# A Mamba block in chunks of 2 and 4 tiles, with its projections, gate inputs, norms and table loads moved

## The chip, the cores and the metric

The kernel runs on one core of one Trainium2 chip, in one launch. The metric is the device time in microseconds (us). The time before is 3584.68 us, the median of three runs (3582.42 to 3585.52). A profile of one execution accompanies it. Engines are named as in the profile: PE is TensorE (PEld its weight loads), DVE is VectorE, ACT is ScalarE, POOL is GpSimd and SP is the queue that issues the DMAs.

## The reference

Four graph layers follow each other on 3327 nodes with 256 features; each is `x = layernorm(x + layer(x, adj))`. The first is a mean aggregation, the third graph attention, the fourth two steps of attention that keeps the largest probabilities. The change lies in the second layer, a graph convolution with a Mamba block behind it:

```
h = layernorm(relu(adj @ x @ gcn_w + gcn_b)) * ln_g + ln_b
xz = h @ w_in                             # 512 channels of xc, 512 of z
xc, z = xz[:, :512], xz[:, 512:]
u = silu(causal 4-tap convolution of xc along the nodes + conv_b)
dbc = u @ w_xp                            # 16 columns for dt, 16 for B, 16 for C
dt = softplus(dbc[:, :16] @ w_dt + b_dt)
for t in nodes:                           # state: 512 channels x 16
    state = exp(dt[t] * A) * state + dt[t] * B[t] * u[t]
    y[t] = state @ C[t]
out = (y + u * D_skip) * silu(z) @ w_out
```

The nodes are the steps of the scan, so that the layer is sequential along them. The convolution of the graph, `adj @ x`, is needed for a node before its step.

## The kernel before

Nodes are padded to 26 tiles of 128. In the second layer channels lie on the partitions, in four groups g of 128, and nodes along the free axis. The nodes are taken in chunks c; `ends` (L261) gives chunks of 1, 2 and 3 tiles and then five of 4 tiles (WC = 512 nodes), eight in all. In each chunk there are 16 slots s, one for each of the state's 16 columns. Slot k = 16c + s does, in the loop at L660:

- `decay` (L571): four ACT exponentials dA = exp(dt * A), one per group, into PSUM. There are two buffers, so that a dA waits until the scan two before it has read its own. `in_turn` (L282) keeps these and a number of other ACT operations in the order of the program.
- `scan` (L585): four DVE scans h = dA * h + (dt u B).
- `feed` (L579): one POOL product of dt u and the row of B, made two slots ahead. `row` (L563) loads the rows of B and C from DRAM by SP, three buffers deep.
- `product` (L592): one DVE product hc of h and the row of C, with two buffers.
- `add_up` (L600): PE transposes that add hc into the sums y of each tile in PSUM. They are issued in the next slot.

Beside this a chunk's slots carry the work for its neighbours, at the slots that `plan(c)` (L246) gives. For chunk c+1 the class `Head` has `project(g)` (two matmuls, an ACT copy and the first tap u on ACT), `taps` (three DVE operations for each group, which read what `project` wrote), `silu`, `mixed` (the product with w_xp), `step_size(g)` (a matmul and two ACT operations), `exponentials` and `logarithms` (softplus), `rounding` and `finish` on DVE, and `skip` (u * D_skip on ACT). For the chunk itself, `gate_input` makes z for one tile; SiLU of the gates follows at slot `gsilu`. For chunk c-1, slot 0 gates the sums (DVE), slots 1 to 4 transpose them and add the residual (`gated`, `residual`), slot 6 makes the factors of the layer norm, and slot 13 applies them to the tiles of X in a loop on ACT (L711). With that `ready` allows `value` (L432), which prepares the third layer for a tile of X, to be used as filling work.

SiLU, exponential and logarithm need different tables on ACT. A table load stands in the program before the first operation that needs another table than the one loaded.

The graph's convolution itself is a generator, `convolve` (L308): for each tile 26 matmuls with the adjacency (loaded by SP in pieces, two buffers), then a chain over ACT and PE for weights, relu and norm, whose last steps (`measure`, `norm`, `turn`) are strewn between the matmuls of the following tile. `turn` writes the transposed tile for `project`. `quota` (L408) spreads this stream over the slots: from `duty`, an estimate of PE's work in each slot in units of about a quarter of a 256-column matmul, it fills the slots evenly, so that the tiles of a chunk are through at the slot of its first projection (`due`, L403); `pump` makes up what is missing. When the stream has ended, `value` takes its place.

Before the first slot, tiles for chunk 0 are convolved, `Head(0)` runs at high priority, and the stream goes on to the end of chunk 1. In the slots (`pinned`) DVE and POOL keep the order of the program; PE and the ACT operations outside `in_turn` are ordered by the scheduler by priority when the program is built, and each engine then takes its own operations strictly in that order. PSUM has one buffer each for projections, gates and residuals together (`ps`) and for convolution and values (`cb`).

After the last slot, the last chunk's four tiles are gated, added and normed one after another, with the values between them (L747 to L766).

Of the kernel before, what the change touches and what calls it, by code (L numbers as in the profile page):

```python
# [9 lines left out]
F32 = mybir.dt.float32  # L10
# [37 lines left out]
def gnn_kernel(ctx: ExitStack, tc: tile.TileContext, n: int, a: dict, out: bass.AP):  # L48
# [109 lines left out]
    with tc.tile_pool(name="l1b", bufs=1) as wpool, tc.tile_pool(name="l1at", bufs=2) as l1at:  # L158
# [33 lines left out]
        with tc.tile_pool(name="l1aw", bufs=1) as cwork, tc.tile_pool(name="l1c", bufs=2) as ch, \  # L192
# [53 lines left out]
            def plan(c):  # L246


                if c == 0:
                    return dict(project={0: (0, 1), 1: (2, 3)}, taps={2: (0, 1), 3: (2, 3)}, gates={2: (0,)}, silu=3, gsilu=3,  # L250
                                mixed=5, sizes={6: (0, 1), 7: (2, 3)}, exps=(8, 9), log=11)
                if c == 1:
                    return dict(project={3: (0, 1), 4: (2, 3)}, taps={5: (0, 1), 6: (2, 3)}, gates={5: (0, 1)}, silu=6, gsilu=6,
                                mixed=8, sizes={8: (0,), 9: (1, 2), 10: (3,)}, exps=(10, 11), log=12)
                return dict(project={6: (0, 1), 7: (2, 3)}, taps={7: (0, 1), 8: (2, 3)}, gates={5: (0, 1), 8: (2,), 12: (3,)},
                            silu=8, gsilu=14, mixed=9, sizes={9: (0,), 10: (1, 2), 11: (3,)}, exps=(11, 12), log=13)

            ends = []
            while not ends or ends[-1] < npad:
                prev = ends[-1] if ends else 0  # L260
                ends.append(min(npad, prev + min(WC, (1 + len(ends)) * P)))  # L261
            nch = len(ends)
            starts = [0] + ends[:-1]
            hTs, us, szs, rows_of = {}, {}, {}, {}
# [17 lines left out]
            def in_turn(op, *x, **k):  # L282
                with tc.issue_after(decays[-1].ins) if decays else nullcontext():
                    decays.append(op(*x, **k))  # L284
# [6 lines left out]
            def power(rs, var):  # L291

                gps.tensor_scalar(rs, var, EPS, None, op0=ALU.add)
                gps.tensor_tensor(rs, rs, mhalf[:, :var.shape[1]], op=ALU.pow)

            def spread(y, sm, nm, sq):

# [10 lines left out]
            def convolve():  # L308
# [3 lines left out]
                for it in range(nt):  # L312
                    cb = cpsum.tile([P, 2, D], F32, name="cb")
                    acc, tp = cb[:, 0, :], cb[:, 1, :]
                    for j in range(nt):
                        if j % JC == 0:
                            m = min(JC, nt - j)
                            at = l1at.tile([P, JC, P], F32, name="at")
                            nc.sync.dma_start(at[:, :m, :], a["adjT"][it][:, j:j + m, :])
                        ten.matmul(acc, at[:, j % JC, :], X0[:, j, :], start=(j == 0), stop=(j == nt - 1))  # L320
                        if j % JM == JM - 1 and j < nt - 1:
                            if rest:
                                step = rest.pop(0)
                                step()
                                full += step is turn
                            yield full, 4 * JM
                    m = cwork.tile([P, D], F32, name="m")
                    act.copy(m, acc)
                    yield full, 8
                    for k in range(2):  # L330
                        ten.transpose(tp[:, k * P:(k + 1) * P], m[:, k * P:(k + 1) * P], ident)
                    mt = cwork.tile([P, D], F32, name="m")
                    act.copy(mt, tp)
                    yield full, 4
                    for k in range(2):
                        ten.matmul(acc, mt[:, k * P:(k + 1) * P], gw[:, k, :], start=(k == 0), stop=False)
                    ten.matmul(acc, one, gb, start=False, stop=True)
                    h = cwork.tile([P, D], F32, name="hn")
                    rs, nb, nm, sm, sq = (small.tile([P, 1], F32, name=x) for x in ("rs", "nb", "nm", "sm", "sq"))
                    act.activation(h, acc, AF.Relu, accum_out=sm)  # L340
                    spread(h, sm, nm, sq)

                    def measure(rs=rs, nb=nb, nm=nm, sq=sq):
                        scales(rs, nb, nm, sq)

                    def norm(h=h, rs=rs, nb=nb):
                        in_turn(act.activation, h, h, AF.Identity, scale=rs, bias=nb)

                    def turn(it=it, h=h):
                        c = next(x for x in range(nch) if it * P < ends[x])  # L350
                        i = it * P - starts[c]
                        if i == 0:
                            hTs[c] = ch.tile([P, D // P, WC], F32, name="hT", bufs=3)
                        pt = psum.tile([P, WC], F32, name="ps")
                        for k in range(2):
                            ten.transpose(pt[:, k * P:(k + 1) * P], h[:, k * P:(k + 1) * P], ident)
                        for k in range(2):
                            act.activation(hTs[c][:, k, i:i + P], pt[:, k * P:(k + 1) * P], AF.Identity,
                                                 scale=g1[:, k:k + 1], bias=b1[:, k:k + 1])
                    rest = [*2 * [lambda: None], measure, *2 * [lambda: None], norm, lambda: None, turn]  # L360
                    if not pinned:
                        for step in (measure, norm, turn):
                            step()
                        rest = []
                        full += 1
                    yield full, 14
# [30 lines left out]
            def tiles_of(c):  # L397
                return (ends[c] - starts[c]) // P if 0 <= c < nch else 0
# [261 lines left out]
            for k, (c, s) in enumerate(states):  # L660
# [6 lines left out]
                if s == 0 and c:  # L667
                    plus = [small.tile([P, WC // P], F32, name=f"{x}c")[:, :tiles_of(c - 1)] for x in ("rs", "nb", "nm", "sm", "sq")]
                if added:
                    add_up(*added)  # L670
                for g in range(NG):
                    scan(k, g, dAs.pop(0))
                    if g < 2:
# [23 lines left out]
                    feed(k + 2)  # L697
                if s == 6 and c:
                    scales(plus[0], plus[1], plus[2], plus[4])
                if s == p["gsilu"]:  # L700
                    in_turn(act.activation, szs[c], szs[c], AF.Silu)
                if after:
                    if s == p["silu"]:
                        ahead.silu()
                    elif s == p["log"]:
                        ahead.logarithms()
                    elif s == 15:
                        ahead.skip()
                    if s in p["exps"]:
                        ahead.exponentials(2 * p["exps"].index(s))  # L710
                if c and s == 13:  # L711
                    rs, nb = plus[:2]
                    for i in range(tiles_of(c - 1)):
                        x = X[:, starts[c - 1] // P + i, :]
                        in_turn(act.activation, x, x, AF.Identity, scale=rs[:, i:i + 1], bias=nb[:, i:i + 1])
                    ready = ends[c - 1] // P

                uses = []
                if c and 1 <= s <= tiles_of(c - 1):
# [854 lines left out]
```

## Time and profile before

| what | value |
|---|---|
| time, median of three runs | 3584.68 us |
| profiled execution | 3579.2 us, span 3577.4 us, granted clock 0.96 |
| busy share of the span: PE, DVE, ACT, POOL | 91%, 67%, 49%, 26% |
| second layer, first convolution to last value | 354.6 to 1451.4 us |
| before the first scan | 354.6 to 416.9 us |
| chunks of 1, 2, 3 tiles (16 slots each) | 68.2, 98.1, 123.3 us |
| chunks of 4 tiles | 152.3, 147.2, 146.9, 146.6, 118.2 us |
| after the last product | 34.2 us |

A chunk is taken here from the end of the last product hc before it to the end of its own last product. Matmuls in fp32 stand as two records each, transposes as one; a busy PE is not at its peak, since the ends of matmuls are modelled and overlap. Starts of consecutive operations are closer than their durations on ACT and DVE, by about 0.1 us. In the timeline, the bracket behind a line gives the idle time of the engine before it and what ended it. Many operations of the slots stand under L277 or L284, the lines of the helpers that record them; they are told apart by their tiles: h is a scan or feed, hc a product, dA a decay, u a tap, X a norm.

### The profile page before, as it was taken

Reading aid. Unit: us, or ns where it says so; the run is one execution under the profiler, and the core shown is the slowest. Engines: PE = TensorE matmul, PEld = TensorE weight load, DVE = VectorE, ACT = ScalarE, POOL = GpSimd, SP = SyncE. Lnnn points to the kernel's source line nnn. Section 1 sums busy time; section 2 is a strip of 40 time slices with the busy share of each in tenths; the row PEclk is TensorE's granted clock in tenths of the full one; section 3 lists DMA queues with packets and bytes.
Section 4 is the critical chain, followed back from the end, with each engine's and each line's share of the span. In section 5 each row is a group of like instructions: output and inputs, shape, how many; then the busy total and the mean of one; then the engine's idle time right before and its main releaser. Section 6 shows DMA issues by size and latency. Waiting matters only on the chain. (4 is left out here: it accounts for less than half of the span.)

```text
span 3577.4 us, 43633 instructions
## 1 busy us (share of the span) xinstructions
PE 3268.2 (91%) x15627; PEld 2564.5 (72%) x15627; DVE 2390.6 (67%) x5342; ACT 1758.9 (49%) x2834; POOL 918.2 (26%) x963
## 2 busy tenths in 40 slices
PE   9999888888888765899989999999998899999996
PEld 7888666666666554688867777878776677777775
DVE  1111378799889898677645454444532999999996
ACT  1000576656667674111133333333335888888883
POOL 0000145455655555111100000000001243333332
PEclk9999999998999987899999999999999999999998
DMA  7443344333333222344321211212122122222220
GB/s 246 141 135 103 95 108 116 105 98 106 102 105 98 60 65 47 123 142 148 110 84 49 63 56 56 64 48 66 53 59 75 44 59 69 65 63 69 69 63 17
DMA packets 151996, 308.01 MB, mean 86 GB/s; under 512 B 19858, under 2 KB 73266, under 8 KB 151634
## 3 DMA queue, kind: packets, MB, share of 16 engines
q1 hardware_dynamic: 151762, 305.06, 29.0%
q8 instruction: 126, 2.06, 0.2%
q14 instruction: 108, 0.88, 0.1%
HBM read 294.36 MB, written 10.65 MB: 85 GB/s over the span
## 5 line engine op out<-in xcount | busy, mean ns | idle before, releaser
L277 POOL TENSOR_TENSOR h<-du,row 128x2048 f32<-128x2048 f32 (+3 forms) x126 | 473.6, 3759 | 447.1 <-DVE hc L277 283.5
L277 DVE TENSOR_TENSOR_SCAN h<-dA,carry,h 128x512 f32<-128x512 f32 (+2 forms) x448 | 492.2, 1151 | 51.7 <-ACT dA L284 51.4
L284 ACT ACTIVATE dA<-t,A_log 128x512 f32<-128x512 f32 (+3 forms) x512 | 308.3, 609 | 174.6 <-DVE h L277 173.3
L1017 PE MATMUL acc<-F,at 128*128 128x256 f32 x1352 | 354.2, 387 | 0.9 <-ACT q L791 0.6
L1050 PE MATMUL acc<-X,wt 128*128 128x256 f32 x1352 | 345.3, 392 | 10.4 <-ACT wt L1048 10.1
L320 PE MATMUL cb<-F,at 128*128 128x256 f32 x1352 | 339.3, 399 | 13.8 <-ACT hn L340 7.5
L1050 PE MATMUL acc<-G,wt 128*128 128x256 f32 x1352 | 336.7, 392 | 5.7 <-ACT wt L981 5.1
L1050 PEld LDWEIGHTS acc<-X,wt 128*128 128x128 f32 x1352 | 244.1, 191 | 105.5 <-issue 41.2
L320 PEld LDWEIGHTS cb<-F,at 128*128 128x128 f32 x1352 | 261.5, 201 | 74.3 <-issue 16.1
L120 PE MATMUL acc<-xa,at 128*128 128x257 f32 x1352 | 308.8, 382 | 5.9 <-DMA at<-in_adjT 5.9
L1017 PE MATMUL acc<-X,at 128*128 128x256 f32 x1352 | 308.1, 381 | 0.0
L926 PE MATMUL acc<-F,at 128*128 128x257 f32 x1352 | 305.7, 383 | 0.6 <-DMA U<-in_U 0.6
L1050 PEld LDWEIGHTS acc<-G,wt 128*128 128x128 f32 x1352 | 250.8, 193 | 65.6 <-ACT wt L981 35.5
L1062 DVE MAX8 cand<-e 128x8 f32<-128x128 f32 x676 | 142.3, 279 | 228.1 <-ACT e L1003 216.4
L1017 PEld LDWEIGHTS acc<-F,at 128*128 128x128 f32 x1352 | 238.4, 191 | 75.1 <-issue 50.2
L120 PEld LDWEIGHTS acc<-xa,at 128*128 128x128 f32 x1352 | 256.1, 191 | 42.5 <-issue 5.9
L604 PE MATMUL y<-ident,hc 128*128 128x128 f32 x1664 | 236.0, 296 | 53.9 <-DVE hc L277 53.7
L1017 PEld LDWEIGHTS acc<-X,at 128*128 128x128 f32 x1352 | 253.3, 191 | 39.4 <-issue 6.6
L926 PEld LDWEIGHTS acc<-F,at 128*128 128x128 f32 x1352 | 255.3, 192 | 36.4 <-issue 1.0
L604 PEld LDWEIGHTS y<-ident,hc 128*128 128x128 f32 x1664 | 210.1, 154 | 92.6 <-DVE hc L277 75.6
L277 DVE TENSOR_TENSOR hc<-h,row 128x2048 f32<-128x2048 f32 (+3 forms) x128 | 245.9, 1921 | 9.3 <-PE y L604 1.3
L1048 ACT COPY wt<-tp 128x512 f32<-128x512 f32 (+1 forms) x182 | 93.6, 557 | 311.2 <-PE tp L1046 311.0
(323 smaller groups left out, 5183.9 us busy)
## 6 DMA issues: line engine op xcount, KB each, us to landing
at<-in_adjT SPq DMA_DIRECT2D x102, 832.0 KB, 4.5
at<-in_adjT SPq DMA_DIRECT2D x260, 320.0 KB, 3.0
row<-bc SPq DMA_DIRECT2D x80, 512.0 KB, 4.9
at<-in_adjT SPq DMA_DIRECT2D x52, 576.0 KB, 3.8
at<-in_adjT SPq DMA_DIRECT2D x26, 512.0 KB, 3.7
row<-bc SPq DMA_DIRECT2D x16, 384.0 KB, 5.1
row<-bc SPq DMA_DIRECT2D x16, 256.0 KB, 4.9
xt<-in_xT SPq DMA_DIRECT2D x26, 128.0 KB, 4.0
```

Of the source, the lines that this page charges most:

```text
L120: nc.tensor.matmul(acc, at[:, j, :], rhs[:, j0 + j, :], start=(j0 + j == 0), stop=(j0 + j == nt - 1))
L277: return lambda *x, **k: tc.keep_in_program_order(op(*x, **k))
L284: decays.append(op(*x, **k))
L320: ten.matmul(acc, at[:, j % JC, :], X0[:, j, :], start=(j == 0), stop=(j == nt - 1))
L604: ten.matmul(y[:, g * P:(g + 1) * P], h[:, g, i * P:(i + 1) * P], ident, is_transpose=True, start=(first and g == 0), stop=(last and g == ...
L926: nc.tensor.matmul(acc, at[:, j, :], F[:, j0 + j, :], start=(j0 + j == 0), stop=(j0 + j == nt - 1))
L1017: nc.tensor.matmul(acc, at[:, j, :], rhs[:, j0 + j, :], start=(j0 + j == 0), stop=(j0 + j == nt - 1))
L1048: copy(wt[:, :m, :], pt[:, :m, :])
L1050: nc.tensor.matmul(acc, wt[:, j, :], rhs[:, j0 + j, :], start=(j0 + j == 0), stop=(j0 + j == nt - 1))
L1062: nc.vector.max(cand[:, s * 8:(s + 1) * 8], z[:, s * SEG:(s + 1) * SEG])
```

## The change

The chunks become 2 tiles and then six times 4 tiles, seven in all, and so 112 slots in place of 128. The plan has two cases: the first chunk prepares the second with one group at each of slots 0 to 3; every other chunk projects at slots 5 and 6 (from 6 and 7 in whole chunks), with the taps at 7 and 8 as in whole chunks before, and makes its gate inputs at 7 and 8, two each (from 5, 5, 8 and 12). SiLU of the gates stands at slot 14 in all chunks. X's norms go one tile to a slot, from slot 9, with `ready` raised by each. After each SiLU and logarithm within the slots a new ACT operation follows, the exponential of one element per partition (`back_to_exp`), so that the table of the exponential is loaded there. Before the slots, the norm of a convolved tile is no longer held to the order of `in_turn`; sums of slot 0 and of the first five slots get high priority from the scheduler.

```diff
                 if c == 0:
-                    return dict(project={0: (0, 1), 1: (2, 3)}, taps={2: (0, 1), 3: (2, 3)}, gates={2: (0,)}, silu=3, gsilu=3,
-                                mixed=5, sizes={6: (0, 1), 7: (2, 3)}, exps=(8, 9), log=11)
-                if c == 1:
-                    return dict(project={3: (0, 1), 4: (2, 3)}, taps={5: (0, 1), 6: (2, 3)}, gates={5: (0, 1)}, silu=6, gsilu=6,
-                                mixed=8, sizes={8: (0,), 9: (1, 2), 10: (3,)}, exps=(10, 11), log=12)
-                return dict(project={6: (0, 1), 7: (2, 3)}, taps={7: (0, 1), 8: (2, 3)}, gates={5: (0, 1), 8: (2,), 12: (3,)},
-                            silu=8, gsilu=14, mixed=9, sizes={9: (0,), 10: (1, 2), 11: (3,)}, exps=(11, 12), log=13)
+                    return dict(project={g: (g,) for g in range(NG)}, taps={g + 2: (g,) for g in range(NG)}, gates={6: (0, 1)},
+                                silu=5, mixed=7, sizes={g + 8: (g,) for g in range(NG)}, exps=(11, 12), log=13)
+                return dict(project={5: (0, 1), 6: (2, 3)}, taps={7: (0, 1), 8: (2, 3)}, gates={7: (0, 1), 8: (2, 3)},
+                            silu=8, mixed=9, sizes={9: (0,), 10: (1, 2), 11: (3,)}, exps=(11, 12), log=13)
...
-                ends.append(min(npad, prev + min(WC, (1 + len(ends)) * P)))
+                ends.append(min(npad, prev + min(WC, (2 + 2 * len(ends)) * P)))
...
+            def back_to_exp():
+                in_turn(act.activation, small.tile([P, 1], F32, name="ex"), eps_t, AF.Exp)
...
                     def norm(h=h, rs=rs, nb=nb):
-                        in_turn(act.activation, h, h, AF.Identity, scale=rs, bias=nb)
+                        turn_or_not = in_turn if pinned else lambda op, *x, **k: op(*x, **k)
+                        turn_or_not(act.activation, h, h, AF.Identity, scale=rs, bias=nb)
...
                 if added:
-                    add_up(*added)
+                    with tc.high_priority() if s == 0 or k < 5 else nullcontext():
+                        add_up(*added)
...
-                if s == p["gsilu"]:
+                if s == 14:
                     in_turn(act.activation, szs[c], szs[c], AF.Silu)
+                    back_to_exp()
                 if after:
                     if s == p["silu"]:
                         ahead.silu()
+                        back_to_exp()
                     elif s == p["log"]:
                         ahead.logarithms()
+                        back_to_exp()
...
-                if c and s == 13:
+                if c and 9 <= s < 9 + tiles_of(c - 1):
                     rs, nb = plus[:2]
-                    for i in range(tiles_of(c - 1)):
-                        x = X[:, starts[c - 1] // P + i, :]
-                        in_turn(act.activation, x, x, AF.Identity, scale=rs[:, i:i + 1], bias=nb[:, i:i + 1])
-                    ready = ends[c - 1] // P
+                    i = s - 9
+                    x = X[:, starts[c - 1] // P + i, :]
+                    in_turn(act.activation, x, x, AF.Identity, scale=rs[:, i:i + 1], bias=nb[:, i:i + 1])
+                    ready = starts[c - 1] // P + i + 1
```

## The prediction

> **What bounds the kernel now.** I read first the busy time by stretch, cut at the starts of the Mamba block's chunks. The columns are length, then busy time and instructions of PE, PEld, DVE, ACT and POOL, the granted clock, the DMA share and GB/s.
>
> ```profile
> core 0: us, PE busy (x) PEld busy (x) DVE busy (x) ACT busy (x) POOL busy (x), PEclk, DMA share, GB/s
> 416.40:484.60 68.20, 60.46 (x273) 45.34 (x272) 46.09 (x97) 49.34 (x141) 24.67 (x23) 0.96 0.36 108
> ...
> 582.70:706.00 123.30, 107.30 (x494) 78.02 (x493) 106.37 (x100) 84.49 (x171) 65.46 (x33) 0.92 0.40 106
> 706.00:858.30 152.30, 125.08 (x614) 94.70 (x613) 132.21 (x101) 95.98 (x181) 81.46 (x33) 0.91 0.37 101
> ...
> 1005.50:1152.40 146.90, 124.78 (x626) 93.81 (x625) 132.56 (x101) 97.53 (x187) 85.86 (x33) 0.94 0.37 105
> ...
> 1417.20:1451.40 34.20, 23.63 (x95) 18.04 (x94) 7.48 (x33) 11.19 (x33) 4.20 (x12) 0.80 0.00 1
> ```
>
> The four lines with a chunk in them are those of 1, 3, 4 and 4 tiles; the last is the end of the block. In a whole chunk DVE is busy 132.6 of 146.9 us: DVE sets the pace and 14.3 us of waiting are open. In the chunks of 1 and 3 tiles DVE is busy 46 of 68 and 106 of 123. Next the waits of DVE in the block, as total, times and longest:
>
> ```profile
> DVE h L277 <- ACT dA L284: 85.7, 44, 20.9
> DVE u L277 <- ACT u L476: 31.4, 10, 7.0
> ```
>
> Then the timeline shows where they lie. In a whole chunk (slot 7 of the one above) DVE ends its scans at 1062.8 and starts the taps 7 us late:
>
> ```profile
> 1057.99 4.80 DVE L277 TENSOR_TENSOR_SCAN h<-dA,carry,h 128x512 f32<-128x512 f32 x4
> 1069.78 2.33 DVE L277 SCALAR_TENSOR_TENSOR u<-t,conv_w,u 128x512 f32<-128x512 f32 x3 [6.98 <-ACT u L476]
> ```
>
> PE, in its order, had waited for a transposed tile and for a gate input before it came to the projection which these taps need:
>
> ```profile
> 1063.49 1.98 PE L552 MATMUL ps<-w_in,hT 128*128 128x512 f32 x4 [2.76 <-ACT hT L358]
> ...
> 1066.15 1.98 PE L473 MATMUL ps<-hT,w_in 128*128 128x512 f32 x4
> ```
>
> In slots 13 and 14 ACT changes its table, works through four X norms of the previous chunk and only then reloads the exponential's table for dA (the scan's decay):
>
> ```profile
> 1124.53 1.28 ACT L284 ACT_TABLE_LOAD   x1 [1.38 <-DVE t L277]
> 1125.82 1.92 ACT L284 ACTIVATE t<-t 128x2048 f32<-128x2048 f32 x1
> 1127.64 2.07 ACT L284 ACTIVATE X<-X,nbc,rsc 128x256 f32<-128x256 f32 x4
> 1129.61 0.58 ACT L284 ACTIVATE hn<-hn,nb,rs 128x256 f32<-128x256 f32 x1
> 1130.21 1.28 ACT L284 ACT_TABLE_LOAD   x1
> 1131.51 1.30 ACT L284 ACTIVATE dA<-t,A_log 128x512 f32<-128x512 f32 x2
> ```
>
> DVE pays for it, and again after the gate's SiLU:
>
> ```profile
> 1132.23 2.46 DVE L277 TENSOR_TENSOR_SCAN h<-dA,carry,h 128x512 f32<-128x512 f32 x2 [3.21 <-ACT dA L284]
> ...
> 1147.59 2.46 DVE L277 TENSOR_TENSOR_SCAN h<-dA,carry,h 128x512 f32<-128x512 f32 x2 [1.42 <-ACT dA L284]
> ```
>
> So a whole chunk has waits of 7.4 us (slot 7), 3.2, 1.4 and about 2 us of small ones.
>
> [...] the trace has the 1283 ns, but the Ln starts 1.29 us after its load starts[...], and I use 1.28. [...] the dA of 512 measures 690[...] (nearest row: a 128x1 ACTIVATE of 198 ns).
>
> **The change part by part.**
>
> *Projections and gates.* The first two projections go from slot 6 to 5, two gate inputs from 5 to 7, one from 12 to 8. In the built program's order PE takes the first projection directly after slot 4's sums, then needs the PSUM buffer that ACT frees with the last residual's X, 1.0 us after slot 6's scans. From there: projection 1.9 (1066.15 above: 1.98 for 4 records), copy 0.55, u 0.75. The inputs of slot 7's first taps are ready some 4.5 us after slot 6's scans, and their second pair at 8.2, when the scans of slot 7 end. ACT's block before slot 7's third dA ends at 5.3, where DVE can use it at 4.65 (product 2.21, two scans 2.45). Wait 0.7 in place of 7.4. SiLU in slot 8 gets a gate copy (0.58) and the extra ACTIVATE (0.2) behind it: dA comes 0.3 late. Without the two slots of cover between projection and taps the old 7 us return.
>
> *X norms spread.* 2.07 us leave slot 13, 0.5 go to each of slots 9 to 12. Behind them on ACT stand the dA. The built order puts before slot 12's third dA: carry 0.1, two dA 1.25, an exponential 0.95, two step-size copies 1.14, the identity 0.95, an X norm 0.5, two more copies 1.17, a copy 0.3, that is 6.4, and the dA ends at 7.05: 2.4 late; a transposed pair between it and the fourth adds 0.5. So a new wait of 2.9 where 0.4 is now. In chunks 1 and 5, whose orders differ, the block is smaller (0.4 and 0.65).
>
> *Table at once.* After Ln: the third dA of slot 14 would end 7.04 us after the scans of slot 13, needed at 7.0: 0.1 in place of 3.2. After the gate's SiLU the load ends 6.2 us after slot 14's scans, dA is needed at 10.4: 0 in place of 1.4. The loads are as many as they were per chunk; they only move ahead of work that needs no table.
>
> A whole chunk: 132.6 busy, waits 0.7 + 0.3 + 2.9 + 0.1, and 1.4 for the small ones: **138**. The chunks that answer to 706.0, 858.3 and 1005.5 are now 152.3, 147.2 and 146.9: 446.4 becomes 414, **-32**. The next one (146.6) keeps its wait at the end of the convolution's stream (4.8 us, a norm behind POOL's product, before dA on ACT) and saves at slots 7, 13 and 14: about 144, **-3**. The last chunk has no head: **0**.
>
> *Chunks of 2 and 4 in place of 1, 2 and 3.* A slot without waits takes 2.29, 3.92, 5.50 and 7.10 us for 1 to 4 tiles (spacing of products), so 6 tiles take 16 x 11.71 = 187 before and 16 x 11.02 = 176 after; taps and step sizes shrink as well. Against that stands the start. Tile 0 is as before up to 374; tile 1 comes without head work: 22 matmuls at 0.433 (two records of 0.217), its chain and transposes, 391. Four projections of 256 columns with convolution between them take 7, and 3.4 more in the clock's halved stretch at 393: 402; taps and SiLU 405. From SiLU to u times D took 15.4 us (381.9 to 397.3) for 128 columns; for 256 I add 0.9 (mixing), 1.6 (step sizes and exponentials), 0.4 (Ln), 2.1 (four DVE operations), 0.4 (skip), 1.5 (tile 2's chain between them on ACT): 427. Table and dA: first scan at **429**, now 417.
>
> Then a new wait. The taps of slot 2 need the first projection of chunk 1, for which tiles 4 and 5 must be through: PE's tile 3 chain ends about 434, each tile takes 13.1 of matmuls and 3 of chain, 467; transposes 4.5, projection, copy and u 3.1: **476**. DVE has done two and a half slots by 440 and waits 36. ACT's order has the same block before slot 3's third dA, so nothing can pass. The row loads behind the adjacency loads on SP's queue, and POOL's products of them, are wanted later than that and hide under it. From there to the end of chunk 0 PE owes: 103 convolution matmuls 45, four chains 7, projections 6.9, gates 3.5, mixing and step sizes 7, sums 12.2: 81 us. DVE owes 13.5 x 3.92 + 8.7 + 9.1 = 71, and the orders of ACT cost it 8 at slot 3, 2.8 at SiLU, 4.3 in slot 12, 3 at Ln and gate, some 5 elsewhere. PE at four fifths, as in the chunks of 1 and 2 tiles (53 and 80 us owed of 68 and 98), takes 100 from 470; DVE comes to 571. Chunk 0 ends at **570**. Chunk 1: 131 busy and 8 of waits, **709**, where six tiles are now done at 706.0: **+3**. Bounds of this part: DVE alone would be done at 547 + 134 = 681 (-25); PE at two thirds 730 (+24).
>
> *Tail.* Each X norm now releases its tile at once, so that four slots earlier values are worked off, and the built order has only four tiles' values after the last sums, the first two behind two residuals. Now PE waits there at every tile:
>
> ```profile
> 1429.14 0.44 PE L436 MATMUL cb<-ident,X 128*128 128x128 f32 x2 [1.87 <-ACT X L760]
> ```
>
> The period is 5.6; without this wait 4.3, three times, and 1.3 at the start: **-5**.
>
> Sum: +3 - 32 - 3 - 5 = -37. The profiled execution (3579.2, span 3577.4) would be 3542. The median of the runs, 3584.68, stands 5.5 above it, and I add that: **3548**.
>
> **The rivals.** (1) The start runs at DVE's pace and not PE's: six tiles at 685 or so, and 3525. For it speaks that PE's waits in the first chunks are partly for ACT; against it ACT's order. Chance 0.15. (2) The waits of slots 7 and 12 are only moved: a late residual X on ACT holds PE before the projection by another 3 us, slot 12 costs 4. Whole chunks are then 143 and the time 3566. For it: PE trails DVE by a slot in the trace (the sums of slot 5 end behind 1065 where the product ended at 1051). Chance 0.17. (3) Slower: the start. PE's one order puts six tiles before slot 2's taps; if PE falls to half its pace there, as its clock does for 6.8 us at a time, chunk 0 costs 45 more and eats all: 470 + 81/0.55 = 617, and 3595 at the end. It decides from 746 for the end of the six tiles. Chance 0.08. (4) The reload does nothing, as when the table had been loaded while waiting: the trace shows the load only after X's norms and the tile norm, and only the SiLU of slot 14 has idle work behind it; without that gain (1.4 in four chunks) it is 3554, within the likeliest case.
>
> **How the numbers follow.** Likeliest 0.6: 3548, from 3535 to 3560. With (1), (2) and (3) the range is 3521 to 3573; beyond it are the slow start and the best of the quick one. A measurement of this kernel tells 0.2% (7 us) from no change. Faster is all of the first case, (1) and (2) but its worst: 0.89; within 0.2%, 0.03; slower 0.08.
>
> **What would show it.** Right: first scan near 429, DVE idle some 36 us in slot 2, six tiles done near 709; whole chunks of 138 with no wait for u in slot 7; no table load between X norms and dA; a wait of 2 to 3 us in slot 12; a period of about 4.3 in the tail. Wrong: whole chunks above 143, or a chunk 0 that ends beyond 600.

## The result

| | before | changed | predicted |
|---|---|---|---|
| median of the runs | 3585.1 us (3582.4 to 3587.4, four runs) | 3561.1 us (3553.1 to 3567.0, four runs) | 3548 (3521 to 3573) |
| ratio to before, 95% interval | | 0.9932, 0.9909 to 0.9955 | 0.990 |
| profiled execution; its span | 3579.2; 3577.4 us | 3553.1; 3551.3 us | 3542 |
| first scan | 416.9 us | 428.1 | 429 |
| six tiles done | 706.0 | 708.4 | 709 |
| the next three chunks, each | 152.3, 147.2, 146.9 us | 143.1, 142.4, 143.0 | 138 |
| the chunk after them, the last chunk | 146.6, 118.2 us | 147.0, 119.1 | 144, 118 |
| after the last product, to the end of the layer | 34.2 us | 25.6 | 29 |

The kernel is faster by 24 us, as forecast in direction, and 13 us slower than the likeliest value. On the spans the change brings 26.1 us: +2.4 for the first six tiles, -17.9 for the three chunks after them, +0.4 and +0.9 for the last two, -8.6 in the tail, and -3.3 outside the layer, which the change does not touch.

The busy time by stretch of the changed kernel, cut at the starts of the chunks; the columns are those of the same view of before. The lines are chunk 0 (2 tiles), chunk 1, one whole chunk, and the tail:

```profile
core 0: us, PE busy (x) PEld busy (x) DVE busy (x) ACT busy (x) POOL busy (x), PEclk, DMA share, GB/s
...
430.60:570.30 139.70, 125.45 (x551) 93.05 (x550) 74.21 (x94) 78.63 (x179) 47.74 (x35) 0.95 0.38 106
570.30:708.40 138.10, 113.85 (x526) 84.19 (x525) 131.68 (x100) 91.30 (x168) 86.25 (x32) 0.89 0.34 99
...
993.90:1136.90 143.00, 128.19 (x625) 97.64 (x624) 132.21 (x101) 97.28 (x190) 88.49 (x34) 0.93 0.39 107
...
1403.00:1428.60 25.60, 19.50 (x89) 14.40 (x89) 7.40 (x32) 9.30 (x27) 4.21 (x12) 0.90 0.00 1
```

In the whole chunk DVE is busy for 132.2 us (132.6 before), and PE for 128.2 in place of 124.8; 10.8 us of DVE's waiting are left, where 14.3 were and 5.4 were forecast. The waits of DVE in the block (total, times, longest):

```profile
DVE h L274 <- ACT dA L281: 57.9, 36, 7.9
DVE u L274 <- issue: 41.0, 1, 41.0
DVE hc L274 <- PE y L605: 12.5, 13, 1.5
DVE u L274 <- ACT u L477: 5.2, 1, 5.2
```

The 31.4 us of waiting for `u` of before are now one wait of 41.0 in chunk 0, plus 5.2 (the profile names no releaser for the 41; PE and ACT were at work on tiles 4 and 5 and the first projection). New is the third line: 13 products that wait until PE has taken up the sums from their buffer. DVE's timeline of the chunk that starts at 993.9 gives the places:

```profile
1031.67 2.29 DVE L274 TENSOR_TENSOR hc<-h,row 128x2048 f32<-128x2048 f32 x1 [1.18 <-PE y L605]
...
1053.88 4.54 DVE L274 SCALAR_TENSOR_TENSOR u<-t,conv_w,u 128x512 f32<-128x512 f32 x6
...
1100.18 1.28 DVE L274 TENSOR_TENSOR_SCAN h<-dA,carry,h 128x512 f32<-128x512 f32 x1 [4.37 <-ACT dA L281]
...
1118.27 2.46 DVE L274 TENSOR_TENSOR_SCAN h<-dA,carry,h 128x512 f32<-128x512 f32 x2 [1.32 <-ACT dA L281]
```

At 1053.88 are slot 7's taps, now six in a row with nothing before them: its 7.4 us are gone, and slot 15 has no wait either. But slots 2, 3, 4 and 6 wait for PE (0.99, 0.53, 1.18, 1.10), slot 12 waits 4.37 and 0.30, and slot 14 still 1.32. Together 9.8. ACT before slot 12's third dA:

```profile
1091.14 0.20 ACT L684 COPY carry<-h 128x4 f32<-128x4 f32 x1
1091.24 1.30 ACT L281 ACTIVATE dA<-t,A_log 128x512 f32<-128x512 f32 x2
1092.48 1.04 ACT L281 ACTIVATE t<-t 128x1024 f32<-128x1024 f32 x1
1093.64 0.69 ACT L513 ACTIVATE t<-ps,b_dt 128x512 f32<-128x512 f32 x1
...
1096.59 1.06 ACT L281 ACTIVATE t<-t 128x1024 f32<-128x1024 f32 x1 [1.69 <-PE ps L512]
1097.55 0.59 ACT L281 ACTIVATE X<-X,nbc,rsc 128x256 f32<-128x256 f32 x1
...
1099.44 0.71 ACT L281 ACTIVATE dA<-t,A_log 128x512 f32<-128x512 f32 x1
```

Ahead of that dA (1099.44) are two dA, step-size copies, two exponential operations and a norm of X. From the carry's copy to the end of the dA this is 7.3 us of work and one wait of 1.69 us. The wait is for PE: the second operation of the exponentials writes a buffer from which the last step-size product still reads (in the built program it waits for PE and for the transfer of the rows of B and C, and both read that buffer). PE gets to that product late:

```profile
1078.29 3.69 PE L498 MATMUL ps<-u,w_sp 128*112 128x512 f32 x8 [0.22 <-ACT sz L555]
...
1092.48 1.12 PE L512 MATMUL ps<-t,w_dt 16*128 16x512 f32 x2
1093.53 1.97 PE L605 MATMUL y<-ident,hc 128*128 128x128 f32 x16
1095.43 1.12 PE L512 MATMUL ps<-t,w_dt 16*128 16x512 f32 x2
```

The kernel before, mixing and last step size on PE and slot 12's third scan on DVE:

```profile
1090.28 3.60 PE L497 MATMUL ps<-u,w_sp 128*112 128x512 f32 x8
...
1104.78 1.12 PE L511 MATMUL ps<-t,w_dt 16*128 16x512 f32 x2
...
1112.70 2.46 DVE L277 TENSOR_TENSOR_SCAN h<-dA,carry,h 128x512 f32<-128x512 f32 x2 [0.41 <-ACT dA L284]
```

The product at 1095.43, the last step size, comes 9.1 us after slot 11's start (1086.3); in the kernel before it came 2.0 us into the slot (1104.78, slot from 1102.8). The sums of slot 10 and twelve convolution matmuls stand ahead of it in both kernels; what differs is when the chain to it begins. PE started the mixing 6.3 us into slot 9 (1078.29), where it had been 1.9 (1090.28, slot from 1088.4). In between lie the four gate inputs of slots 7 and 8; the experiments show that they are not the whole reason.

The tail of the changed kernel on PE:

```profile
1411.50 1.99 PE L626 MATMUL ps<-w_out,gt 128*128 128x256 f32 x8 [0.73 <-ACT gt L617]
1413.33 0.38 PE L437 MATMUL cb<-ident,X 128*128 128x128 f32 x2
...
1414.50 1.04 PE L443 MATMUL cb<-wg,m 128*128 128x258 f32 x4
1415.39 1.99 PE L626 MATMUL ps<-w_out,gt 128*128 128x256 f32 x8
```

The residuals follow each other by 3.9 us (1407.6, 1411.5, 1415.4, 1419.3), where they took 5.6 before and 4.3 were forecast, and the values stand between them without a wait for X.

### The profile page after: what moved, and what is told of

The parts are those of the page before. It is cut to its first block, busy times and chain, and to the rows that moved or that the text cites. A ratio compares the mean times of both kernels' runs of the same rounds, so it can differ in the third digit from the quotient of the medians.

```text
span 3551.3 us, 43260 instructions
## 1 busy us (share of the span) xinstructions
PE 3267.4 (92%) x15595; PEld 2565.1 (72%) x15595; DVE 2370.3 (67%) x5246; ACT 1736.8 (49%) x2743; POOL 931.8 (26%) x942
## 5 line engine op out<-in xcount | busy, mean ns | idle before, releaser
L274 POOL TENSOR_TENSOR h<-du,row 128x2048 f32<-128x2048 f32 (+1 forms) x110 | 467.7, 4252 | 372.5 <-DVE hc L274 297.5
L274 DVE TENSOR_TENSOR_SCAN h<-dA,carry,h 128x512 f32<-128x512 f32 x384 | 466.1, 1266 | 37.7 <-ACT dA L281 37.5
L281 ACT ACTIVATE dA<-t,A_log 128x512 f32<-128x512 f32 (+1 forms) x448 | 292.5, 658 | 153.7 <-DVE h L274 151.2
L320 PE MATMUL cb<-F,at 128*128 128x256 f32 x1352 | 331.0, 395 | 5.1 <-ACT hn L340 5.1
L1067 DVE MAX8 cand<-e 128x8 f32<-128x128 f32 x676 | 142.3, 279 | 228.3 <-ACT e L1008 216.7
L605 PE MATMUL y<-ident,hc 128*128 128x128 f32 x1664 | 243.5, 303 | 35.0 <-DVE hc L274 34.8
L605 PEld LDWEIGHTS y<-ident,hc 128*128 128x128 f32 x1664 | 218.8, 158 | 76.8 <-DVE hc L274 51.4
L274 DVE TENSOR_TENSOR hc<-h,row 128x2048 f32<-128x2048 f32 (+1 forms) x112 | 241.0, 2152 | 18.2 <-PE y L605 12.5
```

Source lines behind the costliest of these rows:

```text
L274: return lambda *x, **k: tc.keep_in_program_order(op(*x, **k))
L605: ten.matmul(y[:, g * P:(g + 1) * P], h[:, g, i * P:(i + 1) * P], ident, is_transpose=True, start=(first and g == 0), stop=(last and g == ...
L1067: nc.vector.max(cand[:, s * 8:(s + 1) * 8], z[:, s * SEG:(s + 1) * SEG])
```

## The experiments

All compare with runs of the kernel before on the same chip. "Block" is the time from the first matmul of the second layer's convolution to the last one of its values, in the profiled execution: 1095.9 before and 1073.1 in the changed kernel. Single executions of one program differ by up to 20 us in one series (3569.9 to 3590.4 in the first run below), so that the block of one execution is a coarse measure as well; the waits inside it repeat much better (slot 12 of the changed kernel waits 4.37 or 4.38 us in five of the six whole chunks of its two profiled executions, 3.66 in the other).

**The plan of before.** Rival accounts were of the plan's worth: nothing, since the waits had only moved, or most of the gain.

```diff
-project={5: (0, 1), 6: (2, 3)}, ... gates={7: (0, 1), 8: (2, 3)}
+project={6: (0, 1), 7: (2, 3)}, ... gates={5: (0, 1), 8: (2,), 12: (3,)}
```

> The changed kernel, but whole chunks keep the plan of before: projections at slots 6 and 7, gate inputs at 5, 8 and 12. Account A, from the trace of the changed kernel: a whole chunk is 143 us = 132.5 busy, 4.7 of waiting for dA in slot 12, 3.8 for PE's sums in slots 2 to 6, 1.3 in slot 14; the first two come from the moved projections and gate inputs, since they hold the mixing and the step sizes back on PE. Undone, the 7.4 of slot 7 return, slot 12 falls to about 1 and the sums to 0.6: 143 again, and the time stays within 4 of the changed kernel's 3561. Account B, the prediction's: the plan is worth 7.4 - 0.7 - 0.3 - 2.5 = 3.9 a chunk, the rest is noise of the profile: about 3577.

Measured: 3575.1 us, ratio 0.9977 (0.9968 to 0.9986). The plan is worth 11 to 16 us (0.9977 less the 0.9932 and 0.9946 of two series of the changed kernel), as account B says, not zero. The places are those of account A, though. DVE in a whole chunk, slots 7, 12 and 15:

```profile
1074.74 2.33 DVE L274 SCALAR_TENSOR_TENSOR u<-t,conv_w,u 128x512 f32<-128x512 f32 x3 [6.99 <-ACT u L477]
...
1118.33 2.46 DVE L274 TENSOR_TENSOR_SCAN h<-dA,carry,h 128x512 f32<-128x512 f32 x2 [0.70 <-ACT dA L281]
...
1151.67 2.46 DVE L274 TENSOR_TENSOR_SCAN h<-dA,carry,h 128x512 f32<-128x512 f32 x2 [1.50 <-ACT dA L281]
```

Slot 7 has its 7.40 back and slot 12 waits 0.70; in the two settled chunks no product waits for PE. These chunks take 145.6 and 145.6 against 142.4 and 143.0. Account A, which had 143, left out slot 15's 1.50 and some waits of 0.2 in other slots. The block is 23 us longer, and the larger part of it lies in the first three chunks (14.1: 145.2, 142.3 and 150.0 where the changed kernel has 142.2, 138.1 and 143.1), which account A did not count; but the profiled execution was the slowest of its series (3590). And slot 15 waits 1.50 although the reload is in this kernel: what took that wait away is the plan.

**No reload.**

```diff
                     in_turn(act.activation, szs[c], szs[c], AF.Silu)
-                    back_to_exp()
```

(and so after the other SiLU and after Ln)

> The changed kernel without the exponential of one element that reloads the table. Account A and the prediction: after Ln nothing changes, since no X norm stands there any more (0.2 us saved); after the gate's SiLU the tile's copies and norms come before the load again and slot 15 waits 1.4, in five chunks: +5 to +7, 3567. Rival: the reload does nothing, 3561, and slot 15 takes 7.1 as with it.

Measured: 3557.2 us, 0.9934 (0.9919 to 0.9949); block 1072.7. The reload is worth nothing that can be measured: the rival. Slot 14 waits 1.25 and slot 15 takes 7.36 with no wait for dA.

**X's norms together.**

```diff
-                if c and 9 <= s < 9 + tiles_of(c - 1):
+                if c and s == 13:
...
-                    i = s - 9
...
+                    for i in range(tiles_of(c - 1)):
...
```

> The changed kernel with the X norms of a chunk together in slot 13, as before; the reload stays ahead of them. Account A: slot 13 (its product to the next) waits 2.1 more for dA, slot 12 0.6 less, in five chunks +8, and the tail takes back its 8: 3577. Rival: the norm that stands in ACT's block before slot 12's third dA is what makes its wait; then that falls by 2 or more, the chunks stay even, and the time is 3569 or less.

Measured: 3561.6 us, 0.9939 (0.9926 to 0.9953); the time is the rival's, for neither's reason. The tail takes back 7.5 us (32.1 against 24.6 from the last product to the last value), so that half of account A holds; but slot 14 waits 1.97, only 0.65 more, slot 15 0.59, and slot 12 2.92 + 0.33. That is 1.4 less than in the changed kernel's trace, but only half of it comes from the norms: slot 11 had the full clock in all three chunks here, and the changed kernel's one chunk with the full clock there (1.00) waits 3.66 + 0.30, 0.7 more. The chunks are even (142.2, 143.5, 143.4; 143.9 for the one at the stream's end, 3 less).

**Both undone.** If either alone hides the other, undoing both must show it.

```diff
-                    back_to_exp()
...
+                if c and s == 13:
...
+                    for i in range(tiles_of(c - 1)):
...
```

> The changed kernel with both undone: X's norms together in slot 13 and no reload. Each alone left slot 14's wait at 1.25 to 1.97. Queue theory: together they restore what the kernel before had there, four norms and the tile's norm between Ln and the table load, 3.2 to 3.4 in slot 14, and 1.4 in slot 15 where the tile's chain stands before the load; with the tail's 7 about 3572. Rival: the reload is worth nothing in any company, and this run equals the one with norms together, 3562 to 3564, slot 14 at 2.

Measured: 3560.5 us, 0.9933 (0.9915 to 0.9951); slot 14 waits 1.88 and slot 15 0.51. The rival again: there was no hidden pair. ACT in slot 13 of this kernel shows why four norms cost so little now:

```profile
1105.08 0.69 ACT L281 ACTIVATE dA<-t,A_log 128x512 f32<-128x512 f32 x1
1105.78 1.28 ACT L281 ACT_TABLE_LOAD   x1
1107.11 1.92 ACT L281 ACTIVATE t<-t 128x2048 f32<-128x2048 f32 x1
1108.92 2.06 ACT L281 ACTIVATE X<-X,nbc,rsc 128x256 f32<-128x256 f32 x4
```

The load of Ln's table stands there at once behind the last dA and runs from 1105.78 while DVE still works on what Ln needs (from 1104.80 to 1107.07; Ln starts at 1107.11). In the kernel before and in the changed one the load is what waits (1.38 us for DVE's `t`), and its 1.28 come after (from 1112.46 in the changed kernel, where DVE's operation ends at 1112.38, and Ln starts at 1113.75). In the built programs the wait for DVE is an instruction of its own ahead of the load in those two, and here it is a part of the Ln, behind the load. So the changed kernel moved the norms out from behind Ln, and kept the load exposed.

**Chunks of before.**

```diff
-ends.append(min(npad, prev + min(WC, (2 + 2 * len(ends)) * P)))
+ends.append(min(npad, prev + min(WC, (1 + len(ends)) * P)))
```

(with the two plans of before for the first two chunks)

> The changed kernel with chunks of 1, 2, 3 and 4 tiles and the two plans of before for the first two of them; whole chunks, norms and reload as changed. Account A: the sizes alone cost the start some time, since PE convolves six tiles before the taps of slot 2 and DVE idles 40 us; six tiles done at about 702 in place of 708, time 3555. Rival: the sizes gain the 11 us by which 6 tiles take less DVE time in two chunks than in three: six tiles done at 718 or later, 3571.

Measured: 3562.4 us, 0.9937 (0.9924 to 0.9950), six tiles done at 711.0. Neither the loss of account A nor the gain of the rival: the sizes of the chunks make no difference that these runs can tell. With the new sizes DVE is busy for 18 us less from the first convolution to the end of the six tiles (221 in place of 239) and ends 2.6 us earlier; the rest goes into its waiting, of which 41 us are one wait.

**The changed kernel again**, for a second profile.

> The changed kernel once more, beside the runs that follow, for a second profile. Its wait for dA in slot 12 took 0.4 to 7 us in the traces so far (4.4 in the changed kernel, 6.0 without the reload, up to 8 with the old chunks). If PE's lateness makes it, it moves again with the granted clock of slots 10 to 12: near 4.4 where that is 0.8 or more in slot 11, near 6 where it is 0.5. If ACT's block of exponentials, copies and norm makes it, it is 4.4 again within 0.3 at any clock. Time 3561 +- 4 either way.

Measured: 3561.0 us, 0.9946 (0.9933 to 0.9959). By itself it decides nothing: slot 11's clock was 0.81 or 0.82 in its three chunks and slot 12 waited 4.37 or 4.38. But in five executions the order of instructions is the same there: these two, the runs without the reload and with the chunks of before, and the last run below. In their fifteen whole chunks between the start and the stream's end (three in each execution) PE either kept the full clock about slot 11 or ran at half clock (0.50) for one stretch:

| half clock | chunks | PE starts the last step size, from slot 11's start | first wait of slot 12 |
|---|---|---|---|
| none | 4 | 8.4 us | 3.66 to 3.68 us |
| 3.4 us | 5 | 9.1 | 4.37 or 4.38 |
| 6.8 us | 5 | 10.75 | 6.03 or 6.04 |
| 10.2 us | 1 | 12.4 | 7.67 |

In every row the wait is PE's start less 4.7. The order is the same in all, so what varies is PE's time, and DVE pays it in full: PE sets the length of slot 12's wait. One chunk of the third row, slots 10 and 11 of the last run below:

```profile
core 0: us, PE busy (x) PEld busy (x) DVE busy (x) ACT busy (x) POOL busy (x), PEclk, DMA share, GB/s
1080.70:1087.80 7.10, 5.88 (x24) 3.15 (x23) 7.01 (x6) 4.88 (x9) 4.52 (x1) 0.99 0.31 83
1087.80:1094.90 7.10, 7.10 (x19) 4.58 (x19) 7.01 (x6) 5.60 (x10) 4.51 (x1) 0.53 0.40 76
```

**The gate inputs of before**, with the projections where the change puts them.

```diff
-gates={7: (0, 1), 8: (2, 3)}
+gates={5: (0, 1), 8: (2,), 12: (3,)}
```

> The changed kernel with the gate inputs of whole chunks at 5, 8 and 12 as before, the projections staying at 5 and 6. PE's theory: the four gate inputs in slots 7 and 8 put off the mixing and the step sizes; with one of them there the last step-size product leaves PE some 4 us earlier in its slot and slot 12 waits 1 to 2 in place of 4.4 to 6; but two gate inputs stand before the projections in slot 5, 2 x 2.0 us of PE and 2 x 0.6 of ACT, so slot 7 gets back 2 to 4: within 5 of 3561. If the lateness has nothing to do with the gate inputs, slot 12 stays above 4 and slot 7 adds its part: 3570.

Measured: 3574.0 us, 0.9978 (0.9971 to 0.9986), chunks 148.0, 147.0, 148.7. Moving the projections alone brings nothing; the plan works only with the gate inputs out of their way. Slot 7 waits 2.49 + 0.55 as expected, but slot 12 waits 4.25, 4.24 and 5.92 and slot 14 2.92: fewer gate inputs in slots 7 and 8 did not shorten slot 12. The first step size does start 5 us earlier on PE, but the last one only 0.3 (8.8 us after slot 11's start where the changed kernel has 9.1, both with a stretch of 3.4 us at half clock). My reason for PE's lateness, the gate inputs, is too narrow: what they leave free was taken by the convolution (32 matmuls in slot 8 and 10 in slot 9, where the changed kernel has 18 and 2), and ACT had a tile's copies in the block as well.

**The convolution shared by length of slot**, and then with the gate inputs later too.

```diff
-busy = [duty(*divmod(i, DS)) for i in range(due(n - 2), due(n - 1))]
+spare = {0: 17, 7: 34, 8: 34, 13: 16, 14: 64}
+busy = [duty(*divmod(i, DS)) - spare.get(i % DS, 0) for i in range(due(n - 2), due(n - 1))]
```

> The changed kernel, but the shares of the convolution count the length of the slots (slots 0, 7, 8, 13 and 14 take 9.3, 11.4, 11.4, 9.2 and 15.3 us, the others 7.1; now each gets its matmuls as if they were equal), so that fewer fall to slots 1 to 6 and 9 to 11 and more to 14. PE's theory: PE's sums in slots 2 to 6 (3.8 us of waiting) are met in time and slot 12 is shorter by 1 or 2: whole chunks 138 to 139, five of them, 3540. ACT's theory: slot 12 keeps its 4.4, the sums go: 3548. If PE was not late at all, nothing: 3561.

> The kernel of the run before this (convolution shared by slot length) with the third and fourth gate inputs at slot 13 in place of 8. PE's theory: the mixing leaves PE 4 us earlier, the last step size too, and slot 12 waits no more than 1; slot 13 carries two gate copies on ACT before the gate's SiLU, 1.2 us that hide under slot 14's long DVE work: whole chunks 135 to 136, 3526. ACT's theory: the block before slot 12's third dA is the same and its wait 4 or more: 3545.

Measured: 3593.8 us, 1.0028 (1.0018 to 1.0038), and 3600.0, 1.0045 (1.0031 to 1.0059): both slower than the kernel before. The first half of the theory holds: in slots 2 to 6 of the last two whole chunks before the stream's end no product waits for PE's sums any more. The second fails: slot 12 waits 9.90 and 11.72. And slot 15, which had no wait, now waits 4.69 and 4.70: the chain of a convolved tile, moved towards slot 14, stands on ACT ahead of its third dA, and its norm waits there for a factor from POOL (3.30 and 2.94). The matmuls meant for slots 7 and 8 were executed in 8 and 9 (26 and 26 in the second kernel), ahead of mixing and step sizes. ACT before slot 12's third dA, in the second:

```profile
1130.60 0.68 ACT L515 ACTIVATE t<-ps,b_dt 128x512 f32<-128x512 f32 x1
1135.52 1.06 ACT L281 ACTIVATE t<-t 128x1024 f32<-128x1024 f32 x1 [4.24 <-PE ps L513]
...
1137.54 0.68 ACT L515 ACTIVATE t<-ps,b_dt 128x512 f32<-128x512 f32 x1
1138.11 1.30 ACT L281 ACTIVATE dA<-t,A_log 128x512 f32<-128x512 f32 x2
```

The same exponential waits 4.24 for the same step-size product, where it was 1.69.

**The step sizes first.** Slot 12's waits in both failures point to one chain: SiLU, mixing, step sizes, exponentials, all before slot 12's third dA.

```diff
-... gates={7: (0, 1), 8: (2, 3)}, ... sizes={9: (0,), 10: (1, 2), 11: (3,)}, ...
+... gates={7: (0, 1), 12: (2, 3)}, ... sizes={9: (0, 1, 2, 3)}, ...
...
-                        uses += [ahead.mixed]
+                        uses += [lambda: first_of_all(ahead.mixed)]
```

(`first_of_all` runs its step under `tc.high_priority()`; the step sizes go through it likewise, and X's norms stand at slots 7, 9, 10 and 12)

> The changed kernel with the chain from mixing to step sizes put first: mixing and step sizes at high priority, all four step sizes at slot 9, the third and fourth gate inputs at slot 12, X's norms at 7, 9, 10 and 12. Queue theory (from the four runs before: the third dA of slot 12 stands on ACT behind the step-size copies and an exponential that waits until PE's last step size has read its buffer, and that step size stands on PE behind sums and convolution): in the built order the last step size now comes before slot 9's sums, and ahead of the third dA of slot 12 there are a carry, a dA, a pair of copies for a tile, two adjacency copies and two exponentials, 4.6 us where the kernel before had 5.0: slot 12 waits 0.5 or less in place of 4.7, slots 2 to 6 keep their 3.8, whole chunks 139, time 3543. Rival: the work on ACT is what it is and the wait only moves, to slots 10, 13 or 14: whole chunks 142 to 144, 3558 to 3565.

Measured: 3580.5 us, 0.9989 (0.9981 to 0.9997), chunks 147.5, 145.5, 148.0. Slot 12 has no wait at all, as the queue theory says. X's norms moved in this run too, but they were worth 0.7 there, so the chain is the cause of the rest. But the rival is right that the wait moves, and the time is longer than even it expected. DVE in slots 9 and 10:

```profile
1090.10 2.46 DVE L274 TENSOR_TENSOR_SCAN h<-dA,carry,h 128x512 f32<-128x512 f32 x2 [4.71 <-ACT dA L281]
...
1104.24 2.29 DVE L274 TENSOR_TENSOR hc<-h,row 128x2048 f32<-128x2048 f32 x1 [4.58 <-PE y L605]
```

and ACT ahead of the dA of slot 9:

```profile
1083.60 1.28 ACT L281 ACT_TABLE_LOAD   x1
1084.89 0.20 ACT L281 ACTIVATE ex<-eps_t 128x1 f32<-128x1 f32 x1
1088.88 0.60 ACT L281 ACTIVATE hn<-hn,nb,rs 128x256 f32<-128x256 f32 x1 [3.79 <-POOL nb L274]
1089.39 1.28 ACT L281 ACTIVATE dA<-t,A_log 128x512 f32<-128x512 f32 x2
```

With the third and fourth gate copies gone, the norm of a convolution tile is next in ACT's order after the reload, its scale comes from POOL, and that is 3.79 late; the dA stand behind it in that order, and DVE waits 4.71 for them; then the step sizes on PE hold up the sums, 4.58.

**The step sizes a slot earlier**, nothing else.

```diff
-sizes={9: (0,), 10: (1, 2), 11: (3,)}
+sizes={9: (0, 1), 10: (2, 3)}
```

> The changed kernel with step sizes at slots 9, 9, 10 and 10 in place of 9, 10, 10 and 11, nothing else. Queue theory: the last step size leaves PE before slot 10's sums, so that the exponential no longer waits 1.7 us for it; but the copies and now also a pair of copies for a tile stand ahead of the third dA: slot 12 waits 3.0 to 3.7 in place of 4.4 to 4.7, 3556. If the wait were ACT's work alone, it would grow by the 1.2 us of the pair and the copy: 5.5, 3565.

Measured: 3555.8 us, 0.9921 (0.9906 to 0.9936); chunks 142.7, 142.1, 144.1. Slot 12 waits 4.37 at clock 1.00 and 6.44 at 0.55, in place of 3.96 and 6.33. The exponential waits no more for PE, but the step-size copies ahead of it do. The wait stays, and neither number was hit: the chain is as long in this order. The time is the queue theory's 3556, but not by its reason, and its interval overlaps those of both series of the changed kernel.

**Ln's table loaded early.** The last open term of the sum: 1.3 us in slot 14.

```diff
                     elif s == p["log"]:
+                        in_turn(act.activation, small.tile([P, 1], F32, name="ex"), eps_t, AF.Ln)
                         ahead.logarithms()
```

> The changed kernel with one thing added: a logarithm of one element ahead of the Ln, which takes nothing from DVE. In the changed kernel's trace the load of Ln's table stands after a wait for DVE's last operation (1.38 us idle, then 1.28 of load), and slot 14's dA is 1.32 late. If that load is what is left of slot 14's wait, it now runs while DVE still works: slot 14 waits 0.1 to 0.3, whole chunks 142, five times 1.2, 3555. If the wait is made by the tile's norm and the second load, as the prediction counted it, slot 14 stays at 1.3 or grows by the 0.2 of the added operation, 3561 to 3562.

Measured: 3552.4 us, 0.9907 (0.9891 to 0.9924), the lowest median of all, though the interval overlaps that of the run before it. ACT in slots 13 and 14:

```profile
1113.51 0.69 ACT L281 ACTIVATE dA<-t,A_log 128x512 f32<-128x512 f32 x1
1114.21 1.28 ACT L281 ACT_TABLE_LOAD   x1
1115.51 0.20 ACT L281 ACTIVATE ex<-eps_t 128x1 f32<-128x1 f32 x1
1115.62 1.90 ACT L281 ACTIVATE t<-t 128x2048 f32<-128x2048 f32 x1
1117.52 1.28 ACT L281 ACT_TABLE_LOAD   x1
```

The load runs at once (in the built program it now stands ahead of the wait for DVE), Ln starts at 1115.62 when DVE's operation has ended (at 1115.50), and slot 14 has no wait (14.22 us long in place of 15.26). The profiled execution, the slowest of its series (3563), had the low clock in slot 11 of the last two of the three chunks (1.00, 0.52 and 0.53), so that these are 143.5 all the same: 1.0 won in slot 14, 1.7 lost in slot 12. The interval of the run lies below that of the second series of the changed kernel and overlaps that of the first by 0.0015.

## Why the prediction was right and where it was wrong

- **The start: right**, step by step: first scan 428.1 (429), the taps of slot 2 at 479.4 (476) after 41 us of idling (36), chunk 0 done at 570.3 (570), six tiles at 708.4 (709). Rival (1) and rival (3) are out. That the new sizes cost or gain nothing agrees with the run with the old ones. Inside chunk 0 there is luck in the sum: from slot 3 on DVE waits 23 us, as the terms of the text add up to, but slot 3 cost 5.2 (8 forecast) and slot 12 7.9 (4.3).
- **Slot 7: right.** 7.4 went to 0 (0.7 forecast), and it takes both moves, as the run with the old gate inputs shows.
- **Whole chunks: 143 and not 138.** Three terms were too small. Slot 12 was put at 2.9 and measured 4.7: "The built order puts before slot 12's third dA" lists ACT's work rightly (7.05 to the dA's end; 7.3 measured), but takes it as if nothing in it waited. The exponential waits 1.7 for PE's last step size, and slot 12's first wait went from 3.7 without half clock to 7.7 with 10.2 us of it. "1.4 for the small ones" stood for waits of the kernel before; the four waits for PE's sums, 3.8, take their place. And "the third dA of slot 14 ... 0.1 in place of 3.2" left out the load of Ln's table, which in this build stands behind the wait for DVE: 1.3. With slots 7 and 8 at 0 this is 138 + 1.8 + 2.4 + 1.2 - 0.7 - 0.3 = 142.4; the other 0.6 is in gaps too short for the list. The text named "whole chunks above 143" as a sign of being wrong, and they lie on that line: 143.1, 142.4 and 143.0, and 143.2, 143.3 and 143.3 in the second profile. The direction and the range held, the account of slots 12 and 14 did not. Rival (2) has the right time, 143 and 3566, and half the mechanism: slot 12 costs 4, but the projection is not held up.
- **Table at once: the wrong cause.** The text gave it 1.4 of slot 15 and the larger part of slot 14. Without the reload the time is the same; slot 15's wait went with the plan. Rival (4) has this right. X's norms spread earn 7.5 us in the tail by the traces and no more; the median with the norms together is the same (3561.6).
- **The chunk at the end of the stream: wrong**, +0.4 for -3. Slots 7 and 13 save 1.5 and 0.3 there and slot 14 nothing. The wait at the end of the stream is 6.3 (slot 2) where it was 5.4 (slot 3), and slots 11 and 12 wait 1.4 and 1.1 where they had no wait. Why was not tried.
- **The tail: right, and larger**, -8.6 for -5: the period is 3.9, and the first values are done between the residuals. The 4.3 of the text did not follow from its own line: 5.6 less the wait of 1.87 is 3.7.
- **The profiled execution against the median**: 5.5 was added, 8.1 measured. That is 2.6 of the 13 us; the other 11 are the chunks (+14.1 in three, +3.4, +0.9), less the start (-0.6), the tail (-3.6) and what lies outside the layer (-3.3).

What stays open: of the 24 us the plan is worth 11 to 16, and the rest is not shown by any run alone; the traces put 8.6 into the tail. Why the chunks that follow the start gain more from the plan than settled ones is open, and so is an order of ACT and PE between slots 8 and 12 without a wait. The attempts that removed the wait they aimed at (the sums', slot 12's) paid elsewhere. A fifth buffer for the exponential, which would take that one wait for PE away alone, was not tried. Nor were two small parts of the change tried alone: the priority of the first sums, and the norm that is no longer held to ACT's order before the slots.

## What to carry to other kernels

A block of work on an engine that keeps its order is only as short as the latest of its inputs (slot 12's third dA: 7.3 us of ACT's work and 1.69 of waiting for PE): when adding up what stands ahead of an instruction, look for the one in the block that waits for another engine or for a buffer, and follow that one back too. Where an engine is busy nearly all the time (PE for 29.2 of 30 us in slots 7 to 9), moving work out of one of its slots lets other queued work move in (with the gate inputs of before, 32 convolution matmuls in slot 8 where there were 18), so the time must be read from the new built order and not from what was moved. A small operation that needs only the next table, put where the engine idles, took the table's load of 1.28 us out of a wait: ahead of Ln, which waits for data, slot 14's wait went from 1.32 us to none. Behind SiLU and Ln it was worth nothing: 3557.2 us without it, 3561 with it.

## What the runs showed of the hardware

The clock that PE is granted in slot 11, 7.1 us with the same order of instructions in five executions, was 1.00, 0.81 to 0.86 or 0.50 to 0.54 on the mean. It was not the same in two executions of the changed kernel: 1.00, 0.86 and 0.83 in the three chunks of the first, 0.82, 0.81 and 0.82 in those of the second. Read in steps of 0.2 us, the clock is either full or half, but for steps in which it changes, and about slot 11 the half clock comes in stretches of 3.41, 6.83 or 10.24 us. In the second layer of the changed kernel's first execution there are 33 stretches at half clock: 15 of 3.41 us, 10 of 6.83, 5 of 10.24 and 3 of 13.65; in the kernel before there are 29, of the same four lengths (6.83 from 393.2, 10.24 from 693.4). All four are multiples of 3.41. What starts and ends a stretch was not shown. Ahead of the stretch at 1085.2 in the changed kernel PE had stood still for no more than 1.2 us at a time since 1045. I had not expected the price: 4.0 us of DVE's time in one chunk between the best and the worst (3.66 and 7.67 in slot 12), though DVE, not PE, has the most work there.

The price of the table load in the prediction, 1.28 us, held: in the last run above the load starts at 1114.21 and the next operation at 1115.51, 1.30 later, and the 42 loads of the changed kernel's second layer took 1.283 us each. In a whole chunk of the kernel before there are six, ahead of the two SiLU (1083.83, 1135.54), of Ln (1124.53) and of the first dA behind each (1088.18, 1130.21, 1145.57); the norms between Ln and dA ran without one of their own. The added exponential of one element took 0.20 us, as the prediction has it; the 128x1 activations of the kernel before took 198 ns.
